# Another order of Strassen's seven products, and gate steps called at other places, in one large fused kernel

## The chip, the cores and the metric

The kernel runs on one core of a Trainium2 chip, as one program. The metric is the device time of one execution in microseconds (us): the median of 3 runs was 2816.5 us, from 2814.86 to 2817.82.

The engines are named as the profile names them. PE is TensorE, the matrix engine; PEld is its loading of weights, which overlaps the matmul before it. DVE is VectorE, ACT is ScalarE, POOL is GpSimd, and SP is SyncE, which here issues most of the transfers (DMA). TensorE writes its results into PSUM, memory in banks of 128 x 512 float32; the other engines read them there and write into SBUF, the chip's working memory (one big tile named `arena` in this kernel).

## The reference

The program is one layer of a model on `x`, 64 sequences of 64 tokens of width 256 (4096 tokens in all), in float32. Each sequence has a type from 0 to 2.

```python
x = x + attn(cond(x, type))
x = x + ffn(cond2(x, type))
```

- `cond`: a gated feed-forward pair (`gelu(x @ W0) * (x @ W1) @ Wo`, 256 to 1024 to 256), once with shared weights and once with weights of the sequence's type. The two results are weighed by a small gate computed from the first token of each sequence.
- `attn`: causal attention with 16 heads of 16, with projections q, k, v and o.
- `cond2`: three shared and two typed feed-forwards (`relu(x @ wi) @ wo`, 256 to 1024 to 256). The typed ones are mixed with fixed weights; the four results are weighed by a second gate that again reads the first tokens.
- `ffn`: a router of three matrices (256 to 1024 to 1024 to 8), the two best of 8 experts for each token, each expert with a capacity; the experts' feed-forwards; and the weighted sum of what they give back.

## The kernel before, in words

**Strassen's scheme.** Nearly all large matrix products are computed with Strassen's scheme in Winograd's form: a product of 2 x 2 blocks in seven block products p1 to p7 instead of eight. The function `strassen` (L210) does this for one product from 256 or more rows of weights into 256 features, for 512 tokens. The weights' sums (`s1` to `s4`) are made beforehand or fetched from memory, the tokens' sums `t1` to `t4` by `token_sums` (L193): t1 and t2 on VectorE or POOL (L195, L196), t3 and t4 on POOL (L197, L198). p1 takes plain blocks, p6 takes t2, p7 takes t3, p5 takes t1, p4 takes t4, p2 and p3 take plain blocks of the tokens. Each block product is four hardware matmuls of 128x256 where the inner size is 256 (a float32 `mm` is two of them), sixteen in the router's second matrix, which has an inner size of 1024.

The results are put together in this way. p1 goes into a bank x1 of PSUM, ScalarE copies it to SBUF (`s1`, L230), and then p2 is added by TensorE in the same bank, which is the block c11. p6 goes into its own bank; VectorE forms u2 = p6 + s1 (L234). p7 into another; u3 = p7 + u2 (L241). p5 into a bank x5; c22 = p5 + u3 (L245); then p3 is added in this same bank, and c12 = x5 + u2 (L249). p4 into a bank; c21 = p4 + u3 (L254). So two banks, x1 and x5, are visited twice, with a read by ScalarE or VectorE in between. `c_done` is called for each finished block (ReLU, or a multiplication by the gate, L298 to L310; in the router L1626). Banks come from a pool of four, and the four accumulators are apart.

**Layers, items, ticks.** `layer` (L281) makes items for a feed-forward: the hidden width is worked through in two to four parts, one item each. An item's `first` does the up product (one scheme; two for the gated pair), then the token sums of the hidden block; its `second` does the down product, in which seven products of four matmuls accumulate over the items in the accumulators `sa` and `sb`, in the order p1, p6, p2, p7, p5, p3, p4. In the last item, ScalarE and VectorE take the results out of the accumulators as they become ready (L349 to L370). `pipeline` (L377) runs first of the next item ahead of second of this one. Small work is put in between: a list `between` holds steps, and `tick()` takes one from it and issues it, with a hint to a scheduler that it come behind the latest of the sums named in `opening`. The steps are those of the sorting of the types (in the cond layers), of the gates (`gate`, L1125: hidden, add_up, logits, spread, then weigh), and of the attention. In `strassen`, a tick follows the products numbered m = 1, 3 and 5 of the scheme (counted from 0), or all but the first with `fine`; in `second`, a tick comes after each pair of products except in the last item.

The order on each engine is not exactly that of the program: a scheduler moves instructions, and each engine then works in its order, waiting on counts of the others' finished instructions. In most schemes the built order is p1, p6, p2, p7, p5, p4, p3.

**The stages**, in order of time, with the names that the tiles have: c (shared gated pair, 8 batches of 512 tokens, two items each), 6.5 to 315 us; a typed repair 315 to 366 us; e (typed gated pair and the attention between), 366 to 859 us; d0 (first shared feed-forward of cond2; batch 4 starts at 1025 us), 859 to 1138 us; d1, 1138 to 1393 us, with another typed repair inside; d2 and t (third shared and typed feed-forwards of cond2, 76.3 us for each batch: two items of d2, then four of t), 1393 to 2009 us; the router's r1 and r2, 2009 to 2533 us; the experts, 2533 to 2810 us.

**Gate steps in d2 and t.** When batch s starts d2, six empty steps and the list of `combine2(s - 1)` (L1425) are put in `between`: hidden, add_up, an empty one, logits, three empty ones, spread, and for each half of the features four weigh steps (L1182), an add, and a step of two adds (L1443), at last `onward`, which issues three fetches of 512 KB on POOL's queue (L1385) for the next batch. The hidden step (tile phb) multiplies the first tokens of the typed result, which eight row fetches on SP's queue (L126, `arena<-spillt`) bring in after the second half of t3, and of the shared results. What is left of the list when the batch's last layer ends is issued at once.

Of the kernel before, what the change touches and what calls it, by code (L numbers as in the profile page):

```python
# [86 lines left out]
def adaln_attn_ffn(ctx: ExitStack, tc: tile.TileContext, a: dict, out: bass.AP):  # L87
# [20 lines left out]
    def bank(name):  # L108
        return psum.tile([P, 512], F32, tag="ps", name=name)
# [97 lines left out]
            y[f"t{n + 1}"] = sums[:, n : n + 1, :]  # L207
        return y, token_sums(eng, eng, y)[1]

    def strassen(name, lhs, rhs, nk, n, width, c_out, c_done, at_st=AT_ST):  # L210

        s1, u2, u3 = (area(at_st + 2 * i, n, width) for i in range(3))

        def product(p, to, first=True, last=True):
            a_, b_ = PRODUCTS[p]
            for i in range(n):
                for k in range(nk):
                    mm(  # L220
                        to[:, i * width : (i + 1) * width], lhs(a_, k, i), rhs(b_, k),
                        first and i == 0 and k == 0, last and i == n - 1 and k == nk - 1, True,
                    )

        def wide(t):
            return t[:, 0 : n * width].rearrange("p (n w) -> p n w", n=n)

        x1 = bank(f"p1{name}")
        product("p1", x1, last=False)
        nc.scalar.copy(s1, wide(x1))  # L230
        yield
        x6 = bank(f"p6{name}")
        product("p6", x6)
        opening[0:1] = [nc.vector.tensor_add(u2, wide(x6), s1).ins]  # L234
        yield
        product("p2", x1, first=False)
        c_done("11", wide(x1))
        yield
        x7 = bank(f"p7{name}")
        product("p7", x7)  # L240
        opening[0:1] = [nc.vector.tensor_add(u3, wide(x7), u2).ins]  # L241
        yield
        x5 = bank(f"p5{name}")
        product("p5", x5, last=False)
        opening[0:1] = [nc.vector.tensor_add(c_out("22"), wide(x5), u3).ins]  # L245
        c_done("22", c_out("22"))
        yield
        product("p3", x5, first=False)
        opening[0:1] = [nc.vector.tensor_add(c_out("12"), wide(x5), u2).ins]  # L249
        c_done("12", c_out("12"))  # L250
        yield
        x4 = bank(f"p4{name}")
        product("p4", x4)
        opening[0:1] = [nc.vector.tensor_add(c_out("21"), wide(x4), u3).ins]  # L254
        c_done("21", c_out("21"))
        yield


    between = []
# [18 lines left out]

        return lambda op, k, i: o[op][:, k, (2 * g + i) * P : (2 * g + i + 1) * P]

    def layer(name, n, ups, down, blocks_of, hops, part, after, ahead=None, at_st=AT_ST, scale=None, at_g=AT_G1, fine=False):  # L281


        acc = {}

        def item(g):
            def first():
                b = blocks_of()
                h = area(hops[nhops[0] % 2], 7, 2, HB)
# [12 lines left out]

                def c_done(ij, src):
                    if gs is not None:
                        nc.vector.tensor_mul(c_out(ij), src, gate_out(ij))
                    elif scale is not None:

                        nc.scalar.activation(c_out(ij), src, AF.Relu, scale=scale(g))
                    else:
                        nc.scalar.activation(c_out(ij), src, AF.Relu)  # L310

                for i, f in enumerate(lhs):
                    to = (gate_out, gate_done) if gs is not None and i == 0 else (c_out, c_done)
                    steps = strassen(f"{name}_{g}{i}", f, lambda op, k: b[op][:, k, :], 1, 2, HB, *to, at_st)
                    for m, _ in enumerate(steps):
                        if m % 2 or fine and m:
                            tick(m not in (1, 4))
                hb = {m: h[:, at] for m, at in NTH.items()}
                opening[:] = token_sums(nc.vector, nc.gpsimd, hb)
                if g == n - 1 and ahead:  # L320
                    ahead()
                return hb

            def second(hb):
                lhs = down(g)
                if g == 0:
                    for i, t in enumerate(pair(f"sa{name}", 0) + pair(f"sb{name}", 1)):
                        acc[i] = t
                last = g == n - 1

                def of(p):
                    i = DOWN[p]
                    return acc[i // 2][:, (i % 2) * HB : (i % 2 + 1) * HB]

                def product(p):
                    a_, b_ = PRODUCTS[p]
                    for k in range(2):
                        mm(
                            of(p), lhs(a_, k), hb[b_][:, k, :],
                            g == 0 and k == 0 and DOWN[p] % 2 == 0,  # L340
                            last and k == 1 and (DOWN[p] % 2 == 1 or p == "p4"), True,
                        )

                s1, u2, u3 = (area(at_st + 2 * i, HB) for i in range(3))
                half = (slice(0, HB), slice(HB, SB))
                for p in ("p1", "p6"):
                    product(p)
                if last:
                    nc.scalar.copy(s1, of("p1"))  # L349
                    nc.vector.tensor_add(u2, of("p6"), s1)  # L350
                else:
                    tick()
                for p in ("p2", "p7"):
                    product(p)
                if not last:
                    tick()
                else:
                    nc.vector.tensor_add(part[:, 0, half[0]], of("p2"), s1)
                    nc.vector.tensor_add(u3, of("p7"), u2)
                for p in ("p5", "p3"):  # L360
                    product(p)
                if not last:
                    tick()
                else:
                    nc.vector.tensor_add(part[:, 1, half[1]], of("p5"), u3)
                    nc.vector.tensor_add(u2, of("p5"), u2)
                    nc.vector.tensor_add(part[:, 0, half[1]], of("p3"), u2)
                product("p4")
                if last:
                    nc.vector.tensor_add(part[:, 1, half[0]], of("p4"), u3)  # L370
                    after()

            return Item(first, second)

        return [item(g) for g in range(n)]
# [408 lines left out]
    def prepare_x(s):  # L784
        if s == 1:
            turn_x(1)
        cut_x(s)
# [249 lines left out]
    def typed1(s, ahead):  # L1037
# [5 lines left out]
        def after():  # L1043
# [343 lines left out]
    def shared2(s, j):  # L1387
# [9 lines left out]
        def down(g):  # L1397
# [214 lines left out]
    def router(s):  # L1612
# [4 lines left out]
        for g in range(2):  # L1617
# [5 lines left out]
            def c_done(ij, src):  # L1623
# [16 lines left out]
        for g in range(2):  # L1640
# [6 lines left out]
            def c_done(ij, src):  # L1647
# [324 lines left out]
```

## Time and profile before

| What | us |
|---|---|
| Median of 3 runs | 2816.5 |
| Lowest and highest run | 2814.86 and 2817.82 |
| The profiled execution's own time | 2820.44 |
| Its span (first to last instruction) | 2818.7 |
| PE busy | 2781.1 (99% of the span), 13881 matmuls |
| DVE busy | 1618.8 (57%) |
| POOL busy | 1033.6 (37%) |
| ACT busy | 843.5 (30%) |
| Granted TensorE clock, mean | 0.995 of full speed |

Busy time by stage, from the windows of the trace:

| Stage (us) | length | PE | DVE | ACT | POOL |
|---|---|---|---|---|---|
| c, 6.5 to 315 | 308.5 | 304.2 | 236.2 | 63.2 | 157.3 |
| e, 366 to 859 | 493.0 | 484.3 | 386.8 | 217.4 | 139.8 |
| d0 to batch 3, 859 to 1025.3 | 166.3 | 161.9 | 127.4 | 68.4 | 86.0 |
| d0 from batch 4, 1025.3 to 1138 | 112.7 | 110.6 | 54.6 | 31.4 | 73.2 |
| d1, 1138 to 1393 | 255.0 | 255.0 | 116.9 | 53.6 | 115.9 |
| d2 and t, 1393 to 2009 | 616.0 | 616.0 | 394.4 | 169.4 | 207.4 |
| router, 2009 to 2533 | 524.0 | 523.9 | 179.5 | 143.0 | 146.5 |
| experts, 2533 to 2810 | 277.0 | 276.6 | 113.4 | 89.6 | 98.9 |

How to read it: the profile is of one execution. Matmuls are pipelined, so the time shown for one reaches into the next, and a matmul that starts late by a few tenths of a microsecond shows in its start and in the idle time of its weight load, hardly in the busy share of PE. In a line of the timeline the first number is the start in us from the span's start, the second the duration, then engine, line, operation, output and inputs, shapes, and in brackets the idle time before it and what ended it. `x4` is four instructions in one line. A line of the waits gives who waited, `<-` for what, the total in us, the number of times and the longest.

### The profile page before, as it was taken

What the parts mean: (1) busy time and instruction counts of PE and PEld (TensorE: products, weight loads), DVE (VectorE), ACT (ScalarE), POOL (GpSimd) and SP (SyncE); (2) the same over time, 40 slices, a digit from 0 to 9 for tenths busy, and PEclk for the clock granted to TensorE, in tenths of its full rate; (3) what the DMA queues carried; (4) which work ended last, traced back from release to release, by engine and by line L of the source; (5) the groups of instructions that cost most, each with busy time, mean ns of one, the idle gap of its engine ahead of it and who ended that gap; (6) DMA issues with size and microseconds to landing.
All of it is one profiled execution on the core that took longest, in us unless ns stands there. A gap on an engine that the chain in (4) does not pass through costs nothing.

```text
span 2818.7 us, 38674 instructions
## 1 busy us (share of the span) xinstructions
PE 2781.1 (99%) x13881; PEld 2255.7 (80%) x13881; DVE 1618.8 (57%) x2925; ACT 843.5 (30%) x1527; POOL 1033.6 (37%) x1057
## 2 busy tenths in 40 slices
PE   9999999999999999999999999999999999999998
PEld 7888877667677778888888888888888888887776
DVE  7877456888887764544446666666543333333443
ACT  2122124544444332211222222222222222222333
POOL 4655122322224557643323323235413323223432
PEclk9999999999999999999999999999999999999999
DMA  4444464333333223553243444444300000013330
GB/s 121 161 154 143 132 223 129 112 110 115 122 110 107 79 89 116 182 190 101 83 177 128 137 137 137 137 137 136 107 16 6 6 6 6 8 33 86 90 98 4
DMA packets 240464, 294.03 MB, mean 104 GB/s; under 512 B 142648, under 2 KB 204944, under 8 KB 240144
## 3 DMA queue, kind: packets, MB, share of 16 engines
q1 hardware_dynamic: 220752, 236.16, 27.3%
q0 software_dynamic: 19296, 54.35, 5.6%
q8 instruction: 110, 1.80, 0.3%
q10 hardware_dynamic: 224, 1.05, 0.1%
q14 instruction: 82, 0.67, 0.1%
HBM read 208.80 MB, written 84.25 MB: 104 GB/s over the span
## 4 chain that ended last, share of the span: by engine, by line
PE 89%; DMA 3%; DVE 3%; issue 2%; SPq 2%; POOL 1%; ACT 0%; POOLq 0%; DVEq 0%; ACTq 0%
PE sad L119 5%; PE p5r L119 5%; PE p1r L119 5%; PE po L119 5%; PE sbd L119 4%; PE sat L119 4%; PE p5d L119 3%; PE sbt L119 3%; PE p1d L119 3%; PE p4r L119 2%; PE p6r L119 2%; PE p7r L119 2%; PE p5t L119 2%; PE p1t L119 2%; PE p5c L119 2%
## 5 line engine op out<-in xcount | busy, mean ns | idle before, releaser
L197 POOL TENSOR_TENSOR arena<-arena 128x512 f32<-128x512 f32 (+1 forms) x175 | 233.8, 1336 | 850.0 <-DVE arena L195 700.4
L198 POOL TENSOR_TENSOR arena<-arena 128x512 f32<-128x512 f32 (+1 forms) x175 | 204.6, 1169 | 30.3 <-DVE arena L196 21.8
L119 PE MATMUL sad<-arena 128*128 128x256 f32 x768 | 176.7, 379 | 0.0
L119 PE MATMUL po<-arena 128*128 128x256 f32 (+1 forms) x704 | 169.8, 399 | 0.1
L119 PEld LDWEIGHTS sad<-arena 128*128 128x128 f32 x768 | 143.7, 190 | 19.1 <-issue 0.8
L119 PEld LDWEIGHTS po<-arena 128*128 128x128 f32 x704 | 132.7, 190 | 28.6 <-issue 11.2
L119 PE MATMUL p5r<-arena 128*128 128x256 f32 x640 | 151.2, 383 | 0.0
L119 PE MATMUL p1r<-arena 128*128 128x256 f32 x640 | 150.1, 381 | 0.0
L119 PEld LDWEIGHTS p5r<-arena 128*128 128x128 f32 x640 | 119.2, 190 | 23.5 <-DVE arena L245 7.5
L1788 POOL DMA_INDIRECT xs<-arena,slot_i x64 | 62.6, 978 | 204.7 <-ACT arena L1784 108.8
L119 PEld LDWEIGHTS p1r<-arena 128*128 128x128 f32 x640 | 119.7, 190 | 21.6 <-issue 5.9
L119 PE MATMUL sbd<-arena 128*128 128x256 f32 x576 | 132.7, 380 | 0.0
L195 DVE TENSOR_TENSOR arena<-arena 128x512 f32<-128x512 f32 (+2 forms) x127 | 97.3, 766 | 59.9 <-ACT arena L310 35.4
L310 ACT ACTIVATE arena<-arena 128x512 f32<-128x512 f32 x144 | 90.4, 630 | 122.6 <-DVE arena L245 90.6
L119 PEld LDWEIGHTS sbd<-arena 128*128 128x128 f32 x576 | 109.1, 190 | 15.2 <-issue 0.4
L119 PE MATMUL sat<-arena 128*128 128x256 f32 x512 | 120.9, 380 | 0.0
L188 POOL TENSOR_TENSOR arena<-arena 128x256 f32<-128x256 f32 (+1 forms) x53 | 48.9, 922 | 192.0 <-DMA arena<-in_L_cond_share_wo 40.2
L196 DVE TENSOR_TENSOR arena<-arena 128x512 f32<-128x512 f32 (+2 forms) x127 | 113.2, 892 | 3.2
L119 PE MATMUL p1d<-arena 128*128 128x256 f32 x384 | 103.9, 393 | 3.5 <-ACT arena L230 2.6
L119 PEld LDWEIGHTS sat<-arena 128*128 128x128 f32 x512 | 96.7, 190 | 13.1
L119 PE MATMUL p5d<-arena 128*128 128x256 f32 x384 | 103.8, 393 | 2.8 <-DVE arena L245 2.8
L1907 POOL DMA_INDIRECT out<-arena,rows_i x40 | 61.9, 1547 | 119.8 <-ACT arena L1906 62.6
(427 smaller groups left out, 6237.1 us busy)
## 6 DMA issues: line engine op xcount, KB each, us to landing
arena<-sums_i SPq DMA_DIRECT2D x32, 896.0 KB
arena<-sums_2i SPq DMA_DIRECT2D x32, 896.0 KB
arena<-sums_2o SPq DMA_DIRECT2D x32, 896.0 KB
arena<-in_L_ffn_eW SPq DMA_DIRECT2D x16, 1024.0 KB
arena<-sums_o SPq DMA_DIRECT2D x16, 896.0 KB
spill<-arena SPq DMA_DIRECT2D x24, 512.0 KB
arena<-spill POOLq DMA_DIRECT2D x24, 512.0 KB, 5.1
sums_i<-arena POOLq DMA_DIRECT2D x12, 896.0 KB, 5.2
```

What stands on the lines that cost most here:

```text
L119: nc.tensor.matmul(o, lhsT=lhsT, rhs=rhs, start=start, stop=stop, skip_group_check=shared_bank)
L188: eng.tensor_add(s1, a21, a22)
L195: eng.tensor_sub(t1, b12, b11)
L196: r = eng.tensor_sub(t2, b22, t1)
L197: eng2.tensor_sub(t3, b22, b12)
L198: return r.ins, eng2.tensor_sub(t4, b21, t2).ins
L310: nc.scalar.activation(c_out(ij), src, AF.Relu)
L1788: nc.gpsimd.indirect_dma_start(out=to.rearrange("e n w -> (e n) w"), out_offset=bass.IndirectOffsetOnAxis(ap=slot_i[:, n, i : i + 1], axis=0),
L1907: nc.gpsimd.indirect_dma_start(out=out_rows, out_offset=bass.IndirectOffsetOnAxis(ap=row_i[:, u : u + 1], axis=0), in_=eo, in_offset=None, ...
```

## The change

`strassen` gets a parameter `late`. With it the order of the products is p6, p1, p7, p5, p2, p4, p3, and VectorE's u2 = p6 + s1 is issued after p1; without it the order is the old one. In the new order two products stand between p1 and p2 (p7 and p5) and between p5 and p3 (p2 and p4). `layer` gets `ticks` in place of `fine`. With "fine" (the e layers, and d0 of batches 0 to 3) order and ticks are the old ones. With "odd" (the c layers) the ticks are the old ones and the order is new, except for the very first scheme. With "late" (all others: d0 from batch 4, d1, d2, t) the order is new, `first` has one tick, after the last product, and `second` has four, after p6, p7, p3 and p4, in the last item too. The router's two schemes take the new order. The schemes of the experts, and the order of products in `second`, stay.

```diff
-    def strassen(name, lhs, rhs, nk, n, width, c_out, c_done, at_st=AT_ST):
+    def strassen(name, lhs, rhs, nk, n, width, c_out, c_done, at_st=AT_ST, late=False):
...
-        x1 = bank(f"p1{name}")
-        product("p1", x1, last=False)
-        nc.scalar.copy(s1, wide(x1))
-        yield
-        x6 = bank(f"p6{name}")
-        product("p6", x6)
-        opening[0:1] = [nc.vector.tensor_add(u2, wide(x6), s1).ins]
-        yield
-        product("p2", x1, first=False)
-        c_done("11", wide(x1))
-        yield
...
+        x = {}
+
+        def p1():
+            x[1] = bank(f"p1{name}")
+            product("p1", x[1], last=False)
+            nc.scalar.copy(s1, wide(x[1]))
+
+        def p6():
+            x[6] = bank(f"p6{name}")
+            product("p6", x[6])
+
+        def sum6():
+            opening[0:1] = [nc.vector.tensor_add(u2, wide(x[6]), s1).ins]
+
+        def p2():
+            product("p2", x[1], first=False)
+            c_done("11", wide(x[1]))
...
+        for fs in (
+            ((p6,), (p1, sum6), (p7,), (p5,), (p2,), (p4,), (p3,)) if late
+            else ((p1,), (p6, sum6), (p2,), (p7,), (p5,), (p3,), (p4,))
+        ):
+            for f in fs:
+                f()
+            yield
...
-    def layer(name, n, ups, down, blocks_of, hops, part, after, ahead=None, at_st=AT_ST, scale=None, at_g=AT_G1, fine=False):
+    def layer(name, n, ups, down, blocks_of, hops, part, after, ahead=None, at_st=AT_ST, scale=None, at_g=AT_G1, ticks="late"):
...
+                    late = ticks != "fine" and (name != "c0" or g + i > 0)
...
-                    steps = strassen(f"{name}_{g}{i}", f, lambda op, k: b[op][:, k, :], 1, 2, HB, *to, at_st)
+                    steps = strassen(f"{name}_{g}{i}", f, lambda op, k: b[op][:, k, :], 1, 2, HB, *to, at_st, late)
                     for m, _ in enumerate(steps):
-                        if m % 2 or fine and m:
+                        if ticks == "fine" and m or ticks == "odd" and m % 2 or ticks == "late" and m == 6:
                             tick(m not in (1, 4))
...
                 if last:
                     nc.scalar.copy(s1, of("p1"))
                     nc.vector.tensor_add(u2, of("p6"), s1)
-                else:
+                if not last or ticks == "late":
                     tick()
                 for p in ("p2", "p7"):
                     product(p)
-                if not last:
-                    tick()
-                else:
+                if last:
                     nc.vector.tensor_add(part[:, 0, half[0]], of("p2"), s1)
                     nc.vector.tensor_add(u3, of("p7"), u2)
+                if not last or ticks == "late":
+                    tick()
                 for p in ("p5", "p3"):
                     product(p)
...
+                if not last or ticks == "late":
+                    tick()
                 product("p4")
+                if ticks == "late":
+                    tick()
                 if last:
                     nc.vector.tensor_add(part[:, 1, half[0]], of("p4"), u3)
                     after()
...
-            (lambda s=s: prepare_x(s + 1)) if s + 1 < NSB else lambda: cut_e(0),
+            (lambda s=s: prepare_x(s + 1)) if s + 1 < NSB else lambda: cut_e(0), ticks="odd",
...
-            lambda: xblocks["e", s], AT_HOPSE, tp1, after, ahead, AT_STE, None, AT_G1E, True,
+            lambda: xblocks["e", s], AT_HOPSE, tp1, after, ahead, AT_STE, None, AT_G1E, "fine",
...
-            lambda: keep2(s, j, part), ahead, (AT_STE, AT_ST, AT_ST2)[j], fine=j == 0,
+            lambda: keep2(s, j, part), ahead, (AT_STE, AT_ST, AT_ST2)[j], ticks="late" if j or s > 3 else "fine",
...
-                lambda op, k: y[op][:, k, :], 1, 2, HB, c_out, c_done,
+                lambda op, k: y[op][:, k, :], 1, 2, HB, c_out, c_done, late=True,
...
-                lambda op, k: h1[op][:, k, :], FH, 2, HB, c_out, c_done,
+                lambda op, k: h1[op][:, k, :], FH, 2, HB, c_out, c_done, late=True,
```

More of the change, by code (lines that the diff above doesn't have):

```diff
@@ L226, in wide @@
             return t[:, 0 : n * width].rearrange("p (n w) -> p n w", n=n)
-        x1 = bank(f"p1{name}")
-        product("p1", x1, last=False)
-        nc.scalar.copy(s1, wide(x1))
-        yield
-        x6 = bank(f"p6{name}")
-        product("p6", x6)
-        opening[0:1] = [nc.vector.tensor_add(u2, wide(x6), s1).ins]
-        yield
-        product("p2", x1, first=False)
-        c_done("11", wide(x1))
-        yield
-        x7 = bank(f"p7{name}")
-        product("p7", x7)
-        opening[0:1] = [nc.vector.tensor_add(u3, wide(x7), u2).ins]
@@ L242, in strassen @@
[L242 to L254, printed above, removed]
@@ L255, in strassen @@
-        c_done("21", c_out("21"))
-        yield
+        x = {}
[11 more added lines that the diff above has]
+            c_done("11", wide(x[1]))
@@ new lines, in p7, with p5, p3 @@
+        def p7():
+            x[7] = bank(f"p7{name}")
+            product("p7", x[7])
+            opening[0:1] = [nc.vector.tensor_add(u3, wide(x[7]), u2).ins]
+        def p5():
+            x[5] = bank(f"p5{name}")
+            product("p5", x[5], last=False)
+            opening[0:1] = [nc.vector.tensor_add(c_out("22"), wide(x[5]), u3).ins]
+            c_done("22", c_out("22"))
+        def p3():
+            product("p3", x[5], first=False)
+            opening[0:1] = [nc.vector.tensor_add(c_out("12"), wide(x[5]), u2).ins]
+            c_done("12", c_out("12"))
@@ L259, in adaln_attn_ffn, with p4 @@
+        def p4():
+            x[4] = bank(f"p4{name}")
+            product("p4", x[4])
+            opening[0:1] = [nc.vector.tensor_add(c_out("21"), wide(x[4]), u3).ins]
+            c_done("21", c_out("21"))
+        for fs in (
[5 more added lines that the diff above has]
+            yield
     between = []
@@ L354, in second @@
                     product(p)
-                if not last:
-                    tick()
-                else:
+                if last:
                     nc.vector.tensor_add(part[:, 0, half[0]], of("p2"), s1)
                     nc.vector.tensor_add(u3, of("p7"), u2)
+                if not last or ticks == "late":
+                    tick()
                 for p in ("p5", "p3"):
                     product(p)
-                if not last:
-                    tick()
-                else:
+                if last:
                     nc.vector.tensor_add(part[:, 1, half[1]], of("p5"), u3)
```

## The prediction

> **What bounds the kernel now.** First the busy times of the page:
>
> ```profile
> PE 2781.1 (99%) x13881; PEld 2255.7 (80%) x13881; DVE 1618.8 (57%) x2925; ACT 843.5 (30%) x1527; POOL 1033.6 (37%) x1057
> ```
>
> TensorE has work in 99% of the span and the change adds and drops no matmul, so it can only win what TensorE loses between matmuls. A short wait hides in "busy": a matmul's span runs into the next. So second the timeline of one scheme of a t layer:
>
> ```profile
> 1494.20 1.03 PE L119 MATMUL p1t<-arena 128*128 128x256 f32 x4
> 1495.06 1.03 PE L119 MATMUL p6t<-arena 128*128 128x256 f32 x4
> 1495.32 0.58 ACT L230 COPY arena<-p1t 128x512 f32<-128x512 f32 x1 [5.61 <-PE p1t L119]
> 1495.95 1.13 PE L119 MATMUL p1t<-arena 128*128 128x256 f32 x4
> 1496.92 1.03 PE L119 MATMUL p7t<-arena 128*128 128x256 f32 x4
> 1498.65 1.03 PE L119 MATMUL p4t<-arena 128*128 128x256 f32 x4
> 1498.90 0.69 DVE L245 TENSOR_TENSOR arena<-p5t,arena 128x512 f32<-128x512 f32 x1 [0.23 <-PE p5t L119]
> 1499.65 1.13 PE L119 MATMUL p5t<-arena 128*128 128x256 f32 x4
> ```
>
> An undisturbed product of four matmuls is followed by the next after 0.86 us (1494.20, 1495.06). The bank p1t is visited twice: p1, then p2 adds into it, after ScalarE has copied p1 out (L230). p5t likewise: p5, then p3, after VectorE's add of L245. In between stands one product, p6 or p4. The chain behind p1 ends at 1495.90, and p2 starts 0.89 after p6 instead of 0.86; then p7 comes 0.97 after p2, since weights that waited are not loaded ahead. So this turnaround, whose weight load sat idle for 0.27, cost 0.03 + 0.11 = 0.14. Behind p5 it is 1.00 and 0.97, so 0.25 for 0.38 of idle. I price a turnaround at its weight-load idle less 0.14. Third, these idles in the waits of the weight loads: cond layers (16 to 315 us), d (1025 to 1420), d2 and t (1420 to 2009), router (2009 to 2533); columns total, times, longest:
>
> ```profile
> PEld p5c L119 <- DVE arena L245: 9.0, 22, 1.7
> PEld p1c L119 <- ACT arena L230: 6.0, 30, 0.3
> ...
> PEld p5d L119 <- DVE arena L245: 9.2, 25, 0.4
> PEld p1d L119 <- ACT arena L230: 9.0, 26, 2.5
> ...
> PEld p5t L119 <- DVE arena L245: 8.6, 25, 0.4
> PEld p1t L119 <- ACT arena L230: 6.7, 25, 0.3
> PEld p5d L119 <- DVE arena L245: 4.4, 14, 0.4
> PEld p1d L119 <- ACT arena L230: 3.7, 14, 0.3
> ...
> PEld p5r L119 <- DVE arena L245: 7.5, 23, 0.4
> ```
>
> **The change part by part.**
>
> *Order.* 135 schemes get p6 p1 p7 p5 p2 p4 p3 (built order: c 31, d0 from batch 4 on 8, d1 16, d2 16, t 32, r1 16, r2 16). Both visits of a bank then have two products between them. Less 0.14 each, the rows come to: c 5.9 + 1.8 = 7.7; d 5.7 + 5.4 = 11.1; t and d2 5.1 + 3.2 + 2.4 + 1.7 = 12.4; router 4.3. Sum 35.5 us. Taking the matmul starts one by one in the same schemes gives 39.8, the upper end.
>
> Does the new chain fit? T is the end of p1. By the rows: ScalarE's copy ends at T + 0.84, u2 (0.69) at 1.55, u3 after 0.10 more at 2.34, the add of p5 at 3.13, TensorE goes on at about 3.19. Four products after p1, at T + 3.46, p3 starts: 0.27 to spare. p2 has 2.59 for the copy's 0.84. Both fit, with little room on VectorE.
>
> What stays: in c a small sorting or unit step of VectorE (0.14 to 0.9 us, one of 1.69) lies between u2 and u3, against 0.27: 3.0 stays. In d the 2.5 wait comes from ScalarE's copy for a store (L1416) that is queued ahead, waiting for POOL: 2.0 stays. In the router 1.2 stays, at second visits that follow a routing product. 35.5 - 6.2 = 29.3 removed.
>
> *New waits of the first product.* p6 needs t2 of its input (L196), p1 only a plain block.
>
> ```profile
> 2217.02 1.06 PE L119 MATMUL prq<-arena,rw 128*32 128x512 f32 x8
> 2217.13 0.69 DVE L249 TENSOR_TENSOR arena<-p5r,arena 128x512 f32<-128x512 f32 x1 [0.36 <-PE p5r L119]
> 2218.01 3.72 PE L119 MATMUL p1r<-arena 128*128 128x256 f32 x16
> 2219.65 1.10 DVE L196 TENSOR_TENSOR arena<-arena 128x512 f32<-128x512 f32 x1
> ```
>
> From r1 to r2, t2 of the second half ends at 2220.75, 3.82 us after r1's last product (2216.93). In the built order p6 and p1 of r2_0 are interleaved: ahead of the matmul that needs this t2 lie prq (1.0), two matmul pairs of p6 (0.86) and four of p1 (1.73): 3.6. So 0.2 in each of 8 batches, 1.6 us. If the scheduled order covered nothing but prq, p6 and half of p1 it would be 1.2, 9.6 us: the upper end; nil is the lower. In c1 and c2 the first p6 waits for POOL's t2 (ends at 45.01 and 83.71, where p1 started at 45.19 and 83.17): 2.0 us at most, taken whole. In other layers this sum is done 5 to 7 us ahead.
>
> *Ticks.* The gate's list (27 entries from hidden to onward) was called at three points of each first half and three of most second halves; now once in first and four times in second. Matmuls of the gate are the same: nil on TensorE. VectorE's weigh steps (L1182, mean 1.17) leave the schemes, where the chain has 0.27 of room, for the down products, where nothing waits for VectorE until the last adds (a cover of a second's seven products, 6 us): nil. The three POOL fetches of onward (L1385, issued from 1549.3 to 1552.3, 5.1 each to landing) move about five products, 4.3 us, later and would land by 1561.7; phb, their first reader, came at 1584.8 and comes some 5 us earlier: 18 to spare, nil; without that cover they would cost up to 4.3 a batch, the size of rival B. POOL's sums queue behind them; POOL stood 4.9 us there for VectorE's adds already, and no row has TensorE waiting for it: nil. The hidden matmuls (phb) move forward against their fetch: rival below. What is left of batch 4's attention (ov7_3, po7) moves from firsts to a second: same matmuls, nil; POOL's and SP's queues keep their order. c's ticks stay at m = 1, 3, 5. In the last item of a layer ticks are new: the s1 copy and VectorE's last adds then stand behind a gate step of at most 1.75. Their readers (the store to spill, the next batch's sums) are over 5 us off, except t3's, whose store heads rival B's chain: nil, at most 1.75 in each of the 7 batches after the first, 12 us, which I count to B.
>
> *Sum.* 29.3 - 1.6 - 2.0 = 25.7 us. The profiled execution took 2820.44 (span 2818.7), 3.9 above the median of 2816.5; so 2794.7 on its footing and **2790.8** on the median's. Own range: all 39.8 won, no new wait, 2776.7; the router's boundary at 9.6 instead of 1.6, 2798.8.
>
> **Rivals.**
>
> *A: VectorE becomes late inside the schemes.* Token sums and weigh steps meet POOL's sums:
>
> ```profile
> 1528.13 0.68 DVE L1182 TENSOR_TENSOR arena<-arena,gwab 128x512 f32<-128x512 f32 x1
> ...
> 1529.84 1.71 POOL L197 TENSOR_TENSOR arena<-arena 128x512 f32<-128x512 f32 x1 [10.01 <-DVE arena L195]
> ...
> 1530.34 4.03 DVE L1182 TENSOR_TENSOR arena<-arena,gwab 128x512 f32<-128x512 f32 x3
> ```
>
> Alone one took 0.68, beside POOL up to 1.75. The new ticks put up to four in a row into a second, right behind the token sums; if they run on into the next scheme, u2 is late and p3 waits. A tail of 1.3 over the slack of 0.27 is 1.0 us, in two schemes of each of 7 batches: 14 us, so 2804.8. For it: the row of three. Against: the adds from PSUM (L234, L241, L245) have means of 689 to 692 ns everywhere, beside POOL or not. [...]
>
> *B: slower, the gate's first step waits for its rows.* phb reads tw, which eight row fetches bring:
>
> ```profile
> 1486.36 10.68 SPq L126 DMA_DIRECT2D arena<-spillt  x8
> ...
> 357.04 3.75 PE L119 MATMUL pel<-arena 128*128 128x256 f32 x8 [4.56 <-DMA arena<-in_L_cond_Wi]
> ```
>
> The second half of t3 ends at 1481.74; phb came at 1508.5 and now comes after 25 products of 0.864, at about 1503.3. The last row lands at 1497.0 + 5.1 (a whole 512 KB fetch) = 1502.1 by a high estimate, at 1498.7 by its semaphore. TensorE works in order, so a late row stops everything. The nearest long wait for a transfer, 4.56 us, also left the clock at 0.76 in 352 to 366 us (1.00 around it) and eight matmuls took 3.75 instead of 1.9. Such a wait in 7 batches: 7 x (4.6 + 1.9) = 45 us, 19 slower than before, 2836. It decides from 4.5 us a batch on. [...]
>
> *C: no change.* A's 14 and the router's 8 together leave 25.7 - 22 = 3.7: 2812.8. That the order isn't built as written is excluded by the built order. But a wait counts all that stands ahead on ScalarE or VectorE, so p2 or p3 could still be held by an unrelated step in these queues.
>
> **How the numbers follow.** Forecast 0.64, A 0.22, C 0.06, B 0.08. About 0.2% (5.6 us) is what can be told from no change here. Faster (below 2810.9): forecast and A, 0.86; same: C, 0.06; slower: B, 0.08. The range of 2776 to 2811 holds the forecast's own range and A, and leaves out B and C.
>
> **What would show it.** Right: the p1 and p5 rows of the weight loads' waits nearly gone from d, t and router, 12 us less in d2 and t, 11 in d, 3 in the router, 4 in c; the adds from PSUM still 0.69. Wrong: p3's loads waiting for L245 in the schemes behind a weigh step (A), an idle time of TensorE before phb released by spillt with a clock under 1.00 (B), or a wait of p6r for L196 of more than 0.2 a batch.

## The result and the profile after

The changed kernel takes 2797.37 us (median of 6 runs, 2795.23 to 2800.29) against 2817.16 of the kernel before (6 runs): a ratio of 0.993, 95% interval 0.9917 to 0.9943, that is 16 to 23 us faster. The profiled execution took 2799.37 us with a span of 2797.7; before it was 2820.44 and 2818.7, so the two profiles are 21.1 apart. The page's busy times:

```profile
PE 2750.0 (98%) x13881; PEld 2269.0 (81%) x13881; DVE 1625.8 (58%) x2925; ACT 834.9 (30%) x1527; POOL 1031.3 (37%) x1057
```

The matmuls are as many, and TensorE is busy 31 us less in a span that is 21 shorter: waits that hid in the time of the matmuls are gone, and some new ones stand openly between them. From the first matmul of one stage to the first of the next, in the two traces (us):

| Stage | before | after | difference | forecast |
|---|---|---|---|---|
| c, with the typed repair | 359.25 | 359.06 | -0.2 | -2.7 |
| e, d0 to batch 3 (order unchanged) | 659.57 | 658.84 | -0.7 | 0 |
| d0 from batch 4, d1 | 367.52 | 357.10 | -10.4 | -9.1 |
| d2 and t | 616.57 | 607.38 | -9.2 | -12.4 |
| router, experts | 800.63 | 799.99 | -0.6 | -1.5 |
| all | 2803.55 | 2782.36 | -21.2 | -25.7 |

One scheme of a t layer in the timeline after:

```profile
1480.92 1.03 PE L119 MATMUL p1t<-arena 128*128 128x256 f32 x4
1481.78 1.03 PE L119 MATMUL p7t<-arena 128*128 128x256 f32 x4
1482.04 0.59 ACT L234 COPY arena<-p1t 128x512 f32<-128x512 f32 x1 [6.47 <-PE p1t L119]
1482.65 1.03 PE L119 MATMUL p5t<-arena 128*128 128x256 f32 x4
1483.51 1.03 PE L119 MATMUL p1t<-arena 128*128 128x256 f32 x4
1484.28 0.69 DVE L255 TENSOR_TENSOR arena<-p5t,arena 128x512 f32<-128x512 f32 x1
1484.37 1.03 PE L119 MATMUL p4t<-arena 128*128 128x256 f32 x4
1485.24 1.03 PE L119 MATMUL p5t<-arena 128*128 128x256 f32 x4
```

Every product now follows the one before after 0.86 or 0.87 us, the second visits of p1t (1483.51) and p5t (1485.24) too. The add of L255 (L245 before) ends at 1484.97, 0.27 before p3's start, which is the room that was forecast. The waits after, for the weight loads, in the same four stages (now c 6 to 315, d 1024.5 to 1381.6, d2 and t to 1989, router to 2510 us):

```profile
PEld p5c L119 <- DVE arena L255: 5.5, 5, 2.1
PEld p6c L119 <- POOL arena L196: 3.3, 2, 2.4
...
PEld p5d L119 <- DVE arena L255: 1.6, 3, 0.9
PEld p4d L119 <- DVE arena L241: 0.9, 1, 0.9
...
PEld phb L119 <- issue: 4.7, 6, 1.7
PEld p5t L119 <- DVE arena L255: 0.4, 1, 0.4
...
PEld p6r L119 <- DVE arena L196: 3.2, 6, 0.5
PEld p5r L119 <- DVE arena L255: 1.1, 2, 0.9
```

The rows of p1 behind ScalarE's copy are gone (one of 0.2 is left in c), that of p5 is left in c (5 long ones instead of 22). New are p6's waits for t2 (L196) in c and in the router, and phb. The waits of the matmuls themselves name what phb waits for in two of its three cases:

```profile
PE phb L119 <- DMA arena<-spillt: 1.8, 2, 1.3
PE phb L119 <- issue: 1.3, 1, 1.3
```

A full batch of d2 and t took 76.28 us before and takes 74.67 now where phb doesn't wait; in three of the seven it does (1.37, 1.35 and 0.55 over its usual delay), 3.3 in all. This wait differs from one execution to the next: in the four other traces below with a new order, the moved ticks and the fetches at this same place it came to 1.1, 1.3, 1.8 and 4.0.

### The profile page after: what moved, and what is told of

It reads as the page before. It is cut to its first block, busy times and chain, and to the rows that moved or that the text cites. A ratio compares the mean times of both kernels' runs of the same rounds, so it can differ in the third digit from the quotient of the medians.

```text
span 2797.7 us, 38593 instructions
## 1 busy us (share of the span) xinstructions
PE 2750.0 (98%) x13881; PEld 2269.0 (81%) x13881; DVE 1625.8 (58%) x2925; ACT 834.9 (30%) x1527; POOL 1031.3 (37%) x1057
## 3 DMA queue, kind: packets, MB, share of 16 engines
q10 hardware_dynamic: 224, 1.05, 0.1%
## 4 chain that ended last, share of the span: by engine, by line
PE 85%; DVE 5%; DMA 4%; issue 3%; SPq 1%; ACT 1%; POOL 1%; POOLq 0%; DVEq 0%; ACTq 0%
PE sad L119 5%; PE p5r L119 5%; PE po L119 5%; PE p1r L119 5%; PE sbd L119 4%; PE sat L119 4%; PE p1d L119 3%; PE p5d L119 3%; PE sbt L119 3%; PE p7r L119 2%; PE p6r L119 2%; PE p4r L119 2%; PE p1e L119 2%; PE p5e L119 2%; PE p5t L119 2%
## 5 line engine op out<-in xcount | busy, mean ns | idle before, releaser
L197 POOL TENSOR_TENSOR arena<-arena 128x512 f32<-128x512 f32 (+1 forms) x175 | 236.5, 1352 | 853.1 <-DVE arena L195 666.0
L198 POOL TENSOR_TENSOR arena<-arena 128x512 f32<-128x512 f32 (+1 forms) x175 | 209.8, 1199 | 29.1 <-DVE arena L196 16.9
L195 DVE TENSOR_TENSOR arena<-arena 128x512 f32<-128x512 f32 (+2 forms) x127 | 95.1, 749 | 57.4 <-ACT arena L331 35.3
L234 ACT COPY arena<-p1d 128x512 f32<-128x512 f32 x48 | 28.1, 586 | 295.3 <-PE p1d L119 291.5
L196 DVE TENSOR_TENSOR arena<-arena 128x512 f32<-128x512 f32 (+2 forms) x127 | 109.7, 864 | 3.2
```

The source lines that it names most:

```text
L195: eng.tensor_sub(t1, b12, b11)
L196: r = eng.tensor_sub(t2, b22, t1)
L197: eng2.tensor_sub(t3, b22, b12)
L198: return r.ins, eng2.tensor_sub(t4, b21, t2).ins
L234: nc.scalar.copy(s1, wide(x[1]))
```

## The experiments

Each kernel was run beside the kernel before on its chip; the ratio is to that. Differences of a few us between these kernels lie inside the intervals, so the stages of the traces carry the finer verdicts, where they repeat: the undisturbed batches of d2 and t in one trace take the same time to 0.02 us, but c and e differ by 4 to 5 us between traces of the same order.

**The order without the ticks.**

```diff
-                        if ticks == "fine" and m or ticks == "odd" and m % 2 or ticks == "late" and m == 6:
+                        if m % 2 or (name[0] == "e" or name[-2:] == "_0") and m:
...
-                if not last or ticks == "late":
+                if not last:
...
-                if ticks == "late":
-                    tick()
```

> The new order in the same 135 schemes, every tick back at its old place. Theory: the order alone removes the turnarounds (about 10 us from batch 4 of d0 to the end of d1, 10 to 12 in d2 and t), and phb, back at its old place, no longer waits for its rows (3.3 us less). But VectorE has only 0.27 us of room inside a scheme, so where a weigh step (1.2) or an add (0.69) of the gate is called between u2 and u3 again, p3 waits about 0.9: some two or three times in each of 7 batches, 10 to 16 us, so d2 and t gain next to nothing and the whole is 2803 to 2810. Rival: VectorE has room enough, the ticks were moved for nothing: d2 and t gain 12 and the whole is 2793 to 2795.

Measured: 2797.18, ratio 0.9918 (0.9904 to 0.9933), the same as the whole change. From batch 4 of d0 to the end of d1: 356.6 (367.5 before), all of the gain. d2 and t: 609.1, a full batch 75.48, between both theories: VectorE's room does bind, in two schemes of each full batch as the theory has it, but the two cost 0.29 and 0.52 and not 0.9 each. The timeline of one of the longer ones, order_only:

```profile
1596.29 0.69 DVE L241 TENSOR_TENSOR arena<-p6t,arena 128x512 f32<-128x512 f32 x1 [1.18 <-ACT arena L234]
1596.90 0.91 DVE L1466 TENSOR_TENSOR arena<-arena 128x512 f32<-128x512 f32 x1
1597.73 0.68 DVE L250 TENSOR_TENSOR arena<-p7t,arena 128x512 f32<-128x512 f32 x1
1598.54 0.69 DVE L255 TENSOR_TENSOR arena<-p5t,arena 128x512 f32<-128x512 f32 x1
1599.29 1.13 PE L119 MATMUL p5t<-arena 128*128 128x256 f32 x4 [0.25 <-DVE arena L255]
```

An add of the gate (L1466) stands between u2 and u3, and p3 starts late. phb, at its old place, doesn't wait. So beside the new order the moved ticks are worth 0.81 in a full batch, 5.0 us over d2 and t, and phb's waits give 3.3 of that back in this pair of traces; the 1.7 that are left are less than two runs of one kernel differ by.

**The ticks without the order** (`late` is False everywhere).

```diff
-                    late = ticks != "fine" and (name != "c0" or g + i > 0)
+                    late = False
...
-                lambda op, k: y[op][:, k, :], 1, 2, HB, c_out, c_done, late=True,
+                lambda op, k: y[op][:, k, :], 1, 2, HB, c_out, c_done,
```

> The old order in all schemes, the ticks at their new places. Theory: moving the ticks gains nothing by itself, since no turnaround of before is longer for a gate step (p5t's longest wait is 0.4), and it brings phb's waits for its rows: 2817 to 2821, with the p1 and p5 rows of the waits as before. Rival: the ticks are what gained: 2805 or less, with d2 and t 9 us shorter than before.

Measured: 2826.03, ratio 1.0021 (1.001 to 1.0033), slower. d2 and t take 621.9, 5.3 more than before. In their waits:

```profile
PEld p5t L119 <- DVE arena L255: 12.1, 32, 0.4
PEld p1t L119 <- ACT arena L234: 8.5, 32, 0.3
```

All 32 schemes of t now have both turnarounds, where 25 had them before: matmuls of the gate (phb and others) used to stand between two visits of a bank and to cover one; now they stand in the down products, where they cover nothing. By matmul starts that is 3.0 of the 5.3; the first weight load of sbd behind phb, idle for 0.4 in each of 7 batches, is 1.3 and phb's waits are 1.0. So the order made the whole gain, and the ticks are worth something only together with it.

**The parts in the router and in c.**

```diff
-                lambda op, k: y[op][:, k, :], 1, 2, HB, c_out, c_done, late=True,
+                lambda op, k: y[op][:, k, :], 1, 2, HB, c_out, c_done,
```

> The changed kernel with the old order in the router's r1 and r2 alone. Theory: in the router the order gives back nearly all that it wins (turnarounds of 4 us less, waits of p6 for token sums of 3.5 more): the router's 8 batches take 0.5 to 1.5 us more than in the changed kernel, the whole 2798 to 2799. Rival: p6 first loses more than it wins there: 1 to 3 us faster than the changed kernel, 2795.

Measured: 2796.22, ratio 0.9913 (0.9898 to 0.9928), which can't be told from the changed kernel. By the trace router and experts take 801.3 with the old order (800.6 before) and 800.0 with the new one, 1.3 for the order; the five traces with p6 first there lie at 799.2 to 800.0, the three with the old order at 800.6 to 801.3. That is the theory's size: the rows of p5r are back (8.0, 23 times), those of p6r for L196 are gone.

```diff
-                    late = ticks != "fine" and (name != "c0" or g + i > 0)
+                    late = ticks == "late"
```

> The changed kernel with the old order in the cond layers alone. Theory: there, too, most is given back (turnarounds 9.7 before against 4.8 after, and 3 us of waits of p6 for POOL's token sums): cond takes 1 to 2 us more than in the changed kernel, the whole 2798 to 2800. Rival: the part is neutral because the 5 us that are left behind p5 come from the order itself and not from the sorting steps between u2 and u3: then these 5 vanish too, and the whole is 2794 to 2797.

Measured: 2797.77, ratio 0.9917 (0.9903 to 0.9932). The waits in c:

```profile
PEld p5c L119 <- DVE arena L255: 9.3, 21, 1.9
PEld p1c L119 <- ACT arena L234: 6.0, 30, 0.3
```

The turnarounds are back and the long ones behind p5c are still there, so these belong to the steps between u2 and u3; the rival falls. c, with the typed repair, takes 361.5 here and 359.1 in the changed kernel. But c varies by itself: with the old order 358.4 to 361.5 in three traces (mean 359.7), with p6 first 357.0 to 361.3 in five (mean 358.4). The gain of some 1.3 us has the right sign and is no more than this scatter.

**Why phb waits.** phb's rows are fetched on SP's queue behind the store of the typed result (`spillt<-arena`). The DMA issues of POOL and SP in the changed kernel:

```profile
1691.69 0.56 POOL L1410 DMA_DIRECT2D arena<-spill  x1
1692.60 1.09 POOL L1410 DMA_DIRECT2D arena<-spill  x2 [0.34 <-DVE arena L1468]
1693.85 1.22 SPq L126 DMA_DIRECT2D spillt<-arena  x2
1703.06 10.06 SPq L126 DMA_DIRECT2D arena<-spillt  x8
```

and the same batch of SP before:

```profile
1711.24 1.23 SPq L126 DMA_DIRECT2D spillt<-arena  x2
1715.23 10.06 SPq L126 DMA_DIRECT2D arena<-spillt  x8
```

Before, the first row was issued 3.99 us after the store; now it is 9.21. The three 512 KB fetches of onward, which used to be issued 6.4 to 10.0 us ahead of the store, now go out 0.7 to 2.5 ahead of it, and by the semaphores the store lands 6.2 to 8.3 us after its issue, in all batches with such fetches, instead of 2.6 to 4.7. The kernel before already has one such case: in its last batch the fetches go out 1.4 to 3.3 us ahead of the store, and the store lands 6.2 to 6.8 us after its issue. To test whether the fetches do it I brought them forward in two ways.

```diff
-        steps = [hidden, add_up, None, logits, None, None, None, spread]
+        steps = [hidden, add_up, None, logits, None, spread]
```

> The changed kernel with two of the three empty steps between the gate's logits and spread taken out, so that everything from spread to the three 512 KB fetches of onward comes two ticks (about 4 us) earlier; phb stays where it is. Theory: phb waits for its rows because these fetches now run at the same time as the store of the typed result, which is ahead of the rows on SP's queue: with the fetches earlier the store lands 2.5 to 4 us after its issue in every batch (3 before, 6 to 9 in the changed kernel), phb never waits, every full batch of d2 and t takes 74.7, and the whole is 2793 to 2795. Rival: the rows are late by their own eight issues, not by the store: phb waits as before, 0.5 to 1.4 in some three batches, 2797.

Measured: 2812.93, ratio 0.9984 (0.9973 to 0.9994): some 15 us worse than the changed kernel. phb waits in no batch and the store lands within 3.7 us, as the theory has it, but the edit broke something that it was not meant to touch:

```profile
PE pgwb L119 <- DVE gwdb L1192: 11.5, 7, 1.6
```

The pause between logits and spread had been covering the softmax on VectorE; without it TensorE waits 1.64 us in each of 7 batches for the spread's input, 11.5 in all, and behind three of these waits its clock was lower (0.55 to 0.65 over the next 3.4 us), some 1.7 us each (last section). The second way keeps that pause and joins the gate's adds instead, two entries less behind the weigh steps:

```diff
-            steps += [add(t0, t0, t1), lambda end=end: [f() for f in end]]
+            steps.append(lambda fs=(add(t0, t0, t1), *end): [f() for f in fs])
```

> The changed kernel with the gate's add and its step of two adds joined in one step for each half of the features: the list is two entries shorter, so the three fetches of onward come two ticks earlier, while logits, spread and the weigh steps of the first half stay where they were (the pause between logits and spread, whose loss cost 12 us in fetch_earlier, is kept). Theory of the collision: the typed store lands within 4 us of its issue, phb never waits, the seven full batches of d2 and t take 74.7 each, 3.3 us less than in the profile of the changed kernel: 2793 to 2795. Rival: three adds in a row on VectorE reach into a scheme or hold the last adds of a layer: 75 to 76 a batch, 2797 or more.

SP's queue in this kernel, the same batch:

```profile
1692.78 1.22 SPq L126 DMA_DIRECT2D spillt<-arena  x2
1696.83 10.05 SPq L126 DMA_DIRECT2D arena<-spillt  x8
```

The rows are issued 4.05 after the store again, and phb waits in no batch; the fetches now go out 9.1 to 11.0 us ahead of the store. So the fetches were the cause. The whole is 2796.73, ratio 0.9915 (0.9899 to 0.9931): no measurable gain, since a full batch takes 74.95 instead of 74.67. Three adds in a row on VectorE cost p3 0.28 a batch, 2 us, and the rival is right about that; d2 and t come to 605.9 against 607.4.

**p1 ahead of p6.** The changed order starts with p6, which needs t2 and so waits in c and in the router. In p1, p6, p7, p5, p2, p4, p3 two or more products still stand between the two visits. Bank x6 is still asked for first, so that p4 gets p6's bank and not p1's.

```diff
-            ((p6,), (p1, sum6), (p7,), (p5,), (p2,), (p4,), (p3,)) if late
+            ((p1,), (p6, sum6), (p7,), (p5,), (p2,), (p4,), (p3,)) if late
...
         def p1():
+            if late:
+                x[6] = bank(f"p6{name}")
             x[1] = bank(f"p1{name}")
...
         def p6():
-            x[6] = bank(f"p6{name}")
+            if not late:
+                x[6] = bank(f"p6{name}")
```

> The changed kernel with p1 ahead of p6: p1, p6, p7, p5, p2, p4, p3; banks as in the changed kernel. Theory: in r2 and in c1 and c2 the first product waits for token sums that p1 does not need, so p6r's waits (2.4 us of matmul starts in the router) and p6c's (3.0) go, and VectorE's room grows from 0.27 to about 0.9, since u2 now starts right after p6 with the copy already done: the 4.8 us behind p5c fall to 1 to 3. Together 4 to 7 us: 2791 to 2794, and d1, d2 and t unchanged. Rival: the router's gain was limited by something else than t2, and the sorting steps are longer than 0.9: 0 to 1.5 us, 2796 to 2797.

Measured: 2787.79, ratio 0.9896 (0.9881 to 0.991), by medians some 10 us faster than the changed kernel, more than expected. In the router p6r's waits for L196 are gone and each batch takes 0.35 to 0.4 less (64.77 against 65.16), 2.4 in eight. c, with the repair, takes 351.7; in six traces of kernels with p1 first 351.2 to 355.9, mean 353.2, against the 358.4 with p6 first: 5 us. Its waits in c:

```profile
PEld p5c L119 <- DVE arena L258: 2.7, 3, 1.6
```

where there were 5.5 behind p5c and 3.3 in p6c. u2 had been waiting for the copy of p1, so counted from p1's end it starts only 0.26 later, while p3 comes one product, 0.86, later: in t's schemes the add of p5 ends 0.78 before p3 instead of 0.27. That is more room for VectorE, which the sorting steps use. d1 and a full batch of t stay within 0.25 us. Router and c make 7 of the 10 us. phb waited 1.1 in this profile instead of 3.3, but as that wait is 1.1 to 4.0 in the traces with the fetches at this place, it isn't shown that the rest comes from there.

**Further versions.** Two put these edits together, and three also take the order with p1 first into more schemes:

> Both edits together: p1 ahead of p6, and the fetches of onward two ticks earlier. Theory: they touch different places, so the gains add: 2788 to 2791, with d2 and t at 74.7 in every full batch. Rival: VectorE's weigh steps, two ticks earlier, now end in a scheme and p3 waits there: 74.9 to 75.5 a batch, no better than p1 ahead alone.

Measured: 2804.26, ratio 0.9952 (0.9939 to 0.9966). What p1 ahead wins is there (c 351.2, a router batch 64.77), and so is the loss of spread's pause (pgwb's 12 us, and the lower clock behind four of the seven waits).

> p1 ahead of p6, and the joined adds. Theory: p1_first had 1.1 us of waits of phb left in its profile; they go, and everything else stays: 1 us less than p1_first, 0.989 of before (2785 to 2788). Rival: the adds in a row cost VectorE's room as above: 0.990 to 0.992.

Measured: 2788.99, ratio 0.9887 (0.9872 to 0.9902): not to be told from p1_first. phb waits nowhere, a full batch takes 74.95; what the one wins the other gives back.

```diff
-                    late = ticks != "fine" and (name != "c0" or g + i > 0)
+                    late = True
...
-                lambda op, k: y[op][:, k, :], 1, 1, HT, c_out, c_done,
+                lambda op, k: y[op][:, k, :], 1, 1, HT, c_out, c_done, late=True,
```

> Both edits, and the order p1, p6, p7, p5, p2, p4, p3 in every scheme, also in e, in d0 of batches 0 to 3, in the very first one and in the experts' (ticks in e and d0 as they are). Theory: the turnarounds that are left there (e 3.8 us, d0 5.0, experts 1.2, the first 0.8) go for the most part: 6 to 9 us less than with the two edits alone, 2780 to 2784. Rival: in e VectorE is 78% busy with attention steps that stand between the sums, so its turnarounds only change their place, and the gain is 0 to 3 us: 2786 to 2790.

Measured: 2809.77, ratio 0.9969 (0.9958 to 0.998), by the medians 5 us worse than p1_first_fetch_earlier, though the intervals overlap. e takes 484.6 (489.0 there), d0's first four batches 175.1 (166.3); another 1.7 of the difference of the two traces is the clock, which fell behind five of the seven waits of pgwb instead of four. In the waits of the matmuls between 360 and 1025 us:

```profile
PE p5e L119 <- DVE arena L1312: 3.8, 5, 1.8
PE pha L119 <- DVE arena L269: 2.9, 1, 2.9
PE px L1442 <- DVE arena L269: 2.8, 1, 2.8
PE sc L119 <- DVE arena L244: 2.1, 2, 1.2
```

There VectorE is behind with its sums (L244, L269), and the gate's and the attention's matmuls wait for them: a place where VectorE has no room to give.

```diff
-                    late = ticks != "fine" and (name != "c0" or g + i > 0)
+                    late = (ticks != "fine" or name[0] == "e") and (name != "c0" or g + i > 0)
```

> The kernel of p1_first_adds_joined with the order p1, p6, p7, p5, p2, p4, p3 in the e layers too (ticks there as they are); d0 of batches 0 to 3 keeps the old order. Theory: in p1_first_all it was d0's early batches that lost (175.1 against 166.4 us, p5 and the attention's matmuls waiting on VectorE's sums), while e took 484.6 against 489 to 494: so this gains 4 to 6 us over p1_first_adds_joined, 0.987 of before (2780 to 2783). Rival: what e won there was only pushed into d0: no gain, d0 of batches 0 to 3 longer by as much.

> p1_first with the order p1, p6, p7, p5, p2, p4, p3 in the e layers too, the gate's adds as in the changed kernel. Theory: the joined adds cost in the schemes (2 us) what the freed store won, so leaving them apart changes nothing by more than 1 us, and e's order wins some 2 to 5: 0.986 to 0.988 of before, as the kernel with the joined adds (0.9878). Rival: the joined adds were what won there and e's order was neutral: 0.9896, as p1_first.

Measured: 2786.41, ratio 0.9878 (0.9862 to 0.9894), with the joined adds, the lowest of all; 2788.51, ratio 0.9893 (0.9876 to 0.9909), without them. d0 keeps its 166.5 and 166.7. e takes 489.1 and 489.6, where it took 489 to 494 with the old order, so that a gain in e is not shown. Without the joined adds phb waited 4.0 in that profile; less the 2 us that the joined adds cost, this is about the difference of these two (2.1). The four versions with p1 first that keep spread's pause and d0's early order can't be told apart from each other; each is faster than the changed kernel, by 8 to 11 us by the medians, and p1_first is the smallest edit of them.

## Why the prediction was right, and where its steps were off

The forecast was 2790.8 with 2777 to 2799 as its own range; 2797.4 was measured, 19.8 won instead of 25.7. The direction and the mechanism hold: ticks_only shows that the order makes the gain, and the timeline shows that it does so by taking the waits between two visits of a bank out. That the time lies within its own range is in part luck: the upper end, 2799, was made with 9.6 us for the router's first product, which took 2.4, and the time went to other places instead, to phb and c.

- *The price of a turnaround, idle less 0.14.* Right where nothing else came in: in d the turnarounds were priced at 11.1, and by matmul starts they took 10.8. What was left there, 2.0, is what stayed (p5d and p4d above). That d gave 10.4 and not 9.1 has another reason. Behind the longest of the removed waits, 2.10 us of TensorE, the clock was at 0.51. This is its end in the kernel before, and the 3.4 us behind it with their granted clock (the last number but two):

```profile
1125.08 1.26 PE L119 MATMUL p1d<-arena 128*128 128x256 f32 x4 [2.10 <-ACT arena L230]
...
1126.00:1129.40 3.40, 3.40 (x9) 2.69 (x9) 1.65 (x4) 0.60 (x1) 2.06 (x3) 0.51 0.68 210
```

The matmuls in these 3.4 us start 0.43 apart instead of 0.22, which cost 1.7 us; in the changed kernel TensorE waits 0.5 us twice in this scheme, before p4 and p3, and the clock stays at 1.00. The prediction's price of a turnaround has no clock in it, so its sum lacks this 1.7.
- *d2 and t, 12.4.* The turnarounds gave that: 9.2 measured and 3.3 lost in phb make 12.5.
- *"The three POOL fetches of onward ... nil".* This step failed, and it is the largest miss. I asked when the fetches' own reader comes (18 us to spare) and not what else they meet on the way. They meet the typed store, whose landing starts the rows for phb. adds_joined shows it.
- *Rival B* is this same wait, priced at 4.6 and more in each of 7 batches, with the clock lower after it. It came at 0.55 to 1.37 in three, and the granted clock around it stayed at 1.00. The bound "the last row lands at 1502.1" was taken in the first batch, which has no such fetches ahead of its store; that one still has 5 us to spare.
- *Ticks, "nil" for the weigh steps.* For the whole change this holds, but the order needs the move: with the ticks at their old places it gave 5.0 us less in d2 and t before phb's waits, as order_only shows. The room of 0.27 on VectorE that the prediction worked out is what a gate step overdraws when it lies in a scheme. I had counted that room and not asked what the order would give without the moved ticks. *Rival A* did not come: with the ticks moved, L255 is late once in d2 and t, by 0.4.
- *Waits of the first product.* The place and the count of matmuls ahead were right. In the router 0.4 in six of eight batches instead of 0.2 in all (2.4 for 1.6), which is one of the signs of being wrong that the prediction named, at a small size; in c 3.0 for 2.0.
- *c, 2.7.* 0.2 in this pair of traces, about 1.3 over the means. The waits behind p5 that stay are 4.8 us by matmul starts, not 3.0. p1_first shows what was lacking: with 0.78 of room instead of 0.27 and no wait of p6 for t2, c takes 5 us less.

## What to carry to other kernels

When an engine reads a bank that the matrix engine will add to, put two products in between instead of one; work out the reader's whole chain from rows, since that decides how much room is left, and keep other work of that engine out of it. Begin with a product whose operands are there anyway. When a transfer is moved, look at what is in flight at its new time and who waits for that, not only at when its own data is needed; and an empty step in a list may be a cover for something. The wait of 2.10 us here cost TensorE 1.7 us more through its clock (0.51 in the 3.4 us behind it), so look at the granted clock behind the long ones.

## What the runs showed of the hardware

A wait of 1.64 us was followed by a lower clock in some batches and not in others. In fetch_earlier TensorE waits the same 1.64 us for pgwb in each of 7 batches. The windows of some 3 us behind it, of TensorE's busy time and granted clock:

```profile
1505.90:1509.00 3.10, 3.10 (x15) 2.75 (x15) 1.48 (x3) 0.00 (x0) 0.00 (x0) 1.00 0.02 5
1658.60:1662.00 3.40, 3.40 (x10) 2.68 (x10) 1.49 (x3) 0.00 (x0) 0.00 (x0) 0.55 0.00 0
1736.60:1740.00 3.40, 3.40 (x12) 2.72 (x12) 1.49 (x3) 0.00 (x0) 0.00 (x0) 0.62 0.00 0
```

The clock is 1.00 in four batches and 0.55, 0.62 and 0.65 in three (the columns behind the length are the busy times of PE, PEld, DVE, ACT and POOL with their counts, then the granted clock). The second one, with its ends put where the clock changes, and its neighbours read:

```profile
1655.51:1658.92 3.41, 1.77 (x9) 1.27 (x8) 2.78 (x5) 0.00 (x0) 2.62 (x2) 1.00 0.33 137
1658.92:1662.33 3.41, 3.41 (x9) 2.66 (x8) 1.29 (x3) 0.00 (x0) 0.00 (x0) 0.50 0.00 0
1662.33:1665.74 3.41, 3.41 (x17) 3.00 (x16) 0.14 (x1) 0.59 (x1) 0.00 (x0) 1.00 0.40 105
```

Here the clock is at 0.50 for 3.41 us, and at 1.00 on both sides. What it costs stands in the timeline of two batches, the first without and the second with the lower clock:

```profile
1505.92 2.86 PE L119 MATMUL sbt<-arena 128*128 128x256 f32 x12
...
1658.62 4.54 PE L119 MATMUL sbt<-arena 128*128 128x256 f32 x12
```

The same twelve matmuls take 1.7 us more, about as much as the wait itself. The three waits of phb in the changed kernel, 1.30 us at most, left the clock at 1.00.

In the two other traces with this wait of 1.64 us in seven batches, the lower clock came behind four of the seven (p1_first_fetch_earlier) and behind five (p1_first_all). What sets these batches apart from the others isn't shown: the wait is as long in all of them.

Two of the small VectorE steps in that chain took longer beside POOL's sums than without them. The same profile, fetch_earlier:

```profile
1656.87 1.26 POOL L198 TENSOR_TENSOR arena<-arena 128x512 f32<-128x512 f32 x1
1656.96 1.21 DVE L1192 TENSOR_TENSOR gwdb<-gwb,ident 8x32 f32<-8x32 f32 x1
```

The operation of L1192, on 8x32 elements, takes 1.21 us beside POOL's sum of 128x512, which takes 1.26; in the last batch of this profile, with no POOL operation beside it, the same operation took 0.18. The step ahead of it (L1189, 8x4, one tensor and one value for each partition) took 1.05 beside L197, and 0.22 in that last batch. The reciprocal of 8x1 ahead of that took 0.14, beside L197.
